# The edge stage of a graph layer in fp32: TensorE's products grouped by the shape that they take of the array, and vector messages that carry the zero score

## Chip, cores and metric

One core of one Trainium2 chip runs the whole program. The metric is the device time of one execution in microseconds (us), the median of several; lower is better. All tensors are fp32, and so are all TensorE products. Each of them leaves two records in the trace (a transpose leaves one), so 416 products of one kind stand there as x832.

## The reference, cut to what matters

A layer over a graph of 3125 nodes (256 features each) and 53125 edges that are sorted by their target node. It adds a message-passing block and a linear-attention block to `x`, and then a mixture of 8 experts. The change lies in the message-passing block alone. For each edge, after the linear maps are folded together:

```python
r  = edge_vector / |edge_vector|                     # 3 numbers for each edge
z  = [x0[src] , sum_m x1[src][:, m] * r[m]]          # 64 + 64 features of the source node
h  = z @ Wab                                         # 64 numbers, hidden scalars
sc = leaky_relu(h, 0.01) @ Wsc                       # 64 scores
act = softmax([sc, 0, 0, ... 0])                     # 256 wide: 192 scores are zero
msg[0:64]   = act[0:64] * (z @ Wo)[0:64]
msg[64:256] = act_zero  * ((z @ Wo)[64:128] (x) r + Q[src])   # one common zero score
agg[dst] += msg                                      # segment sum over the edges
```

The softmax has one common weight for its 192 zero scores. With `ex` the exponentials and `z` one over their sum, a scalar message has the factor `ex[u] * z`, and a vector message the factor `ex[U] * z`, where `ex[U]` is the exponential of the zero score (`U` is 64).

## The kernel before, in words

Three stages follow one another. Up to about 78 us the node table is written (`table`, 448 numbers a node: features and `Q`). From there to about 692 us runs the edge stage, `edges` (L762), which the change touches. The experts (`blocks`, L1253) follow to the end; their first block's products start as the edge stage ends.

The edge stage works on 104 groups of 4 x 128 edges. Group `s` goes through these functions, spread over four iterations of the loop at L947:

- `gather` (L786): four indirect DMAs issued by GpSimd (POOL) fetch the table rows of 512 source nodes into `xg`. Seven buffers; the gather runs three groups ahead.
- `features` (L810): three VectorE (DVE) operations build the second half of `z` in `xg`: `tmp<-xg`, `tmp<-tmp`, `xg<-tmp`.
- `places` (L794): `place`, a one-hot matrix of each edge's node in a window of 64 nodes.
- `turn` (L817): four TensorE transposes into `pz`, which ScalarE (ACT) copies to `zT`. These take all 128 rows and 128 columns of the array.
- `products` (L824): `ph` (the hidden scalars: 128 rows, 64 columns of the array, two products into the two halves of the partitions), from which ACT makes `little`, and `eo` (z @ Wo: four products of 128 x 128). `eo` has two PSUM buffers.
- `second_layer` (L840): `low` on DVE (the leaky relu), then four products `sc` (64 rows, 128 columns).
- `scores` (L853): `nm` on DVE, then four exponentials `ex` on ACT, with their sums in `z`.
- `messages` (L864): four small operations on `z`, then `zplace` on ACT (four operations, `place` times the zero weight) and `oplace` on DVE (`place` times `z`), then the messages `msg`, vectors (768 wide) and scalars (256 wide).
- `sums` (L894): products that add the messages into `ps`, 64 nodes x 256, for two halves of the partitions (128 rows, 64 columns). For each of two halves `b`: `msg`'s scalars with `oplace` (64 wide), `msg`'s vectors with `zplace` (192 wide), `Q` from `xg` with `zplace` (192 wide). In the first half of a window's first group all of `msg` goes with `oplace` in one product of 256 columns, because that product has to start the sum; for these tiles alone the vector messages are multiplied by `ex[U]` beforehand (`weight`, `re`).
- A window has three groups. At its end one product (`ps<-win,move`, L921) adds what the window before holds of this one, ACT copies the sum out (`win`, L929), and `second` (L934) does the same for the other half (64 rows, 64 columns). The `win` rows go to `agg` in HBM over SyncE's queue.

One iteration traces, in this order: `gather(s+3)`, `sums(s-3)`, a step of side work (attention, gate and planning of the experts: its products are named `gp`), `scores(s-2)`, `features(s)`, `places(s)`, `turn(s)`, `second_layer(s-1)`, `messages(s-2)`, `products(s)`, `second(s-3)`. The order on each engine is then set by a scheduler that takes what is ready first by its own estimates; `tc.issue_after(x)` binds it to put an instruction behind `x` on the same engine. It is an order of issue, not a wait. Before the change `ph(g)` is bound behind `sc(g-1)`, `sc(g)` behind the transposes of `g+1`, `low(g)` behind the features of `g+1`, and the `z` of `g` behind `low(g+1)`. The scheduler also splits the four transposes in two pairs in places.

Of the kernel before, what the change touches and what calls it, by code (L numbers as in the profile page):

```python
# [9 lines left out]
F32 = mybir.dt.float32  # L10
# [7 lines left out]
P = 128  # L18
# [8 lines left out]
def tile_gps_layer(  # L27
# [16 lines left out]
    nc = tc.nc  # L44
    N, D = x.shape
    NE = src.shape[0]
    U = 64
# [5 lines left out]
    G = 4  # L53
    JT = -(-NE // (P * G)) * G
    NG = JT // G
# [6 lines left out]
    TW = D + 3 * U  # L62
# [4 lines left out]
    W = 64  # L67
# [26 lines left out]
    ident = const.tile([P, P], F32, name="ident")  # L94
# [7 lines left out]
    wab = const.tile([P, U], F32, name="wab")  # L102
    wo = const.tile([P, 2 * U], F32, name="wo")
# [5 lines left out]
    r3 = const.tile([P, 3, JT], F32, name="r3")  # L109
# [40 lines left out]
    order = keep_.tile([P, EX], F32, name="order")  # L150
# [611 lines left out]
    def edges(gps):  # L762
        with tc.tile_pool(name="xgp", bufs=7) as xgp, tc.tile_pool(name="sp", bufs=5) as spool, \
# [5 lines left out]
                tc.tile_pool(name="sps", bufs=1, space=PSUM) as sps, \  # L769
                tc.tile_pool(name="gwork", bufs=1) as gw:  # L770
            XG, S, ZT, EO, MSG, WIN, SUM, MOVE = {}, {}, {}, {}, {}, {}, {}, {}
            READY_, HEAD, LOW, LSC, TURN, SC, M1 = {}, {}, {}, {}, {}, {}, {}
            ENDS = {}
            LAST = []
            both_sums = sps.tile([P, 2, D], F32, name="ps")
            WIN[-1] = spool.tile([P, D], F32, name="win", bufs=3)
            nc.gpsimd.memset(WIN[-1], 0.0)
            weight = spool.tile([P, G], F32, name="weight", bufs=1)
            nc.vector.memset(weight, 1.0)

            def pair(g):

                v = (g + 1) // 3
                return v, g - max(0, 3 * v - 1), 3 if v else 2
# [31 lines left out]

            def turn(g):  # L817
                pz = zps.tile([P, G, P], F32, name="pz")
                for i in range(G):
                    TURN[g] = nc.tensor.transpose(pz[:, i, :], XG[g][:, i, 0:P], ident)  # L820
                ZT[g] = ew.tile([P, G, P], F32, name="zT", bufs=3)
                nc.scalar.copy(ZT[g], pz)  # L822

            def products(g):  # L824

                zT = ZT.pop(g)
                ph = hps.tile([P, 2 * P], F32, name="ph")
                for h in range(2):
                    with tc.issue_after(LSC[g - 1].ins) if g and not h else nullcontext():
                        nc.tensor.matmul(ph[h * U:(h + 1) * U, :], lhsT=wab,  # L830
                                         rhs=zT[:, 2 * h:2 * h + 2, :].rearrange("p t e -> p (t e)"),
                                         start=True, stop=True)
                little = ew.tile([P, 2 * P], F32, name="little")
                nc.scalar.activation(little, ph, AF.Copy, scale=0.01)
                LOW[g] = ph, little
                EO[g] = eo = ops.tile([P, G, 2 * U], F32, name="eo")
                for t in range(G):
                    nc.tensor.matmul(eo[:, t, :], lhsT=zT[:, t, :], rhs=wo, start=True, stop=True)  # L838

            def second_layer(g):  # L840
                ph, little = LOW.pop(g)
                low = ew.tile([P, 2 * P], F32, name="low")
                with tc.issue_after(READY_[g + 1].ins) if g + 1 < NG else nullcontext():
                    LOW[g] = nc.vector.tensor_tensor(low, ph, little, OP.max)
                SC[g] = sc = cps.tile([P, G, 4 * U], F32, name="sc")
                with tc.issue_after(TURN[g + 1].ins) if g + 1 < NG else nullcontext():
                    for b in range(2):
                        for h in range(2):
                            hs = slice(h * U, (h + 1) * U)
                            LSC[g] = nc.tensor.matmul(sc[:, 2 * h + b, 0:U + 1], lhsT=low[hs, b * P:(b + 1) * P],  # L850
                                                      rhs=lsc[hs, :], start=True, stop=True)
# [9 lines left out]
                                         bias=nm[:, i:i + 1], accum_out=z[:, i:i + 1])  # L861
                HEAD[g] = ex, z

            def messages(g):  # L864
                eo, place = EO.pop(g), S.pop(g)
                ex, z = HEAD.pop(g)
                order = LOW[g + 1] if g + 1 < NG else None
                with tc.issue_after(order.ins) if order else nullcontext():
                    nc.vector.scalar_tensor_tensor(z, ex[:, :, U], float(3 * U - 1), z, op0=OP.mult, op1=OP.add)
                nc.vector.reciprocal(z, z)  # L870

                zero = ew.tile([P, G], F32, name="zero")
                nc.vector.tensor_mul(zero, z, ex[:, :, U])  # L873
                zero_place = spool.tile([P, G, W], F32, name="zplace", bufs=3)
                for i in range(G):
                    nc.scalar.activation(zero_place[:, i, :], place[:, i, :], AF.Copy, scale=zero[:, i:i + 1])  # L876
                one_place = spool.tile([P, G, W], F32, name="oplace", bufs=3)
                order = nc.vector.tensor_mul(one_place, place, z.unsqueeze(2).to_broadcast([P, G, W]))
                msg = ew.tile([P, G, D], F32, name="msg", bufs=3)
                rg = r3[:, :, g * G:(g + 1) * G].rearrange("p m g -> p g m")  # L880
                if pair(g)[1] == 0:

                    re = ew.tile([P, G, 3], F32, name="re")
                    nc.vector.tensor_copy(weight[:, 0:G:2], ex[:, 0:G:2, U])
                    nc.vector.tensor_mul(re, rg, weight.unsqueeze(2).to_broadcast([P, G, 3]))
                    rg = re
                with tc.issue_after(order.ins):
                    nc.vector.tensor_mul(msg[:, :, U:D].rearrange("p g (u m) -> p g u m", m=3),  # L888
                                         eo[:, :, U:2 * U].unsqueeze(3).to_broadcast([P, G, U, 3]),
                                         rg.unsqueeze(2).to_broadcast([P, G, U, 3]))  # L890
                nc.vector.tensor_mul(msg[:, :, 0:U], eo[:, :, 0:U], ex[:, :, 0:U])  # L891
                MSG[g] = msg, one_place, zero_place

            def sums(g):  # L894
                msg, one_place, zero_place = MSG.pop(g)
                v, q, n = pair(g)
                if q == 0:
                    SUM[v] = both_sums[:, v & 1, :]
                ps = SUM[v]
                xg = XG.pop(g)  # L900
                for b in range(2):

                    whole = q == b == 0
                    for what in range(3):
                        if whole and what == 1:
                            continue
                        for h in range(2):
                            i = 2 * h + b
                            hs = slice(h * W, (h + 1) * W)

                            with tc.issue_after(ENDS[v - 1].ins) if v and h and whole and not what else nullcontext():
                                if what == 0:
                                    c1 = D if whole else U
                                    nc.tensor.matmul(ps[hs, 0:c1], lhsT=one_place[:, i, :], rhs=msg[:, i, 0:c1],  # L914
                                                     start=whole, stop=False)
                                else:
                                    nc.tensor.matmul(ps[hs, U:D], lhsT=zero_place[:, i, :],  # L917
                                                     rhs=msg[:, i, U:D] if what == 1 else xg[:, i, D:TW],
                                                     start=False, stop=False)
                if q == n - 1:  # L920
                    nc.tensor.matmul(ps[0:W, :], lhsT=MOVE[v][:, 0, :], rhs=WIN.pop(v - 1),  # L921
                                     start=False, stop=True)
                    WIN[v] = spool.tile([P, D], F32, name="win", bufs=3)
                    close(v, 0)

# [8 lines left out]
            def second(g):  # L934
                v, q, n = pair(g)
                if q == n - 1:
                    ENDS[v] = nc.tensor.matmul(SUM[v][W:P, :], lhsT=MOVE.pop(v)[0:W, 1, :], rhs=WIN[v][0:W, :],  # L937
                                               start=False, stop=True)
                    close(v, 1)
                    del SUM[v]  # L940

# [5 lines left out]
            for s in range(NG + 3):  # L947
# [9 lines left out]
                    scores(s - 2)  # L957
                if s < NG:
                    features(s)
                    places(s)  # L960
                    turn(s)
                if 1 <= s < NG + 1:
                    second_layer(s - 1)
                if 2 <= s < NG + 2:
                    messages(s - 2)
                if s < NG:
                    products(s)
                if 3 <= s:
                    second(s - 3)

# [426 lines left out]
```

## Time and profile before

| | before |
|---|---|
| median of 3 runs | 1110.63 us (1109.84 to 1115.06) |
| profiled execution | 1108.81 us, span 1106.9 us, mean granted TensorE clock 0.964 |
| TensorE (PE) busy | 1018.8 us, 92% of the span |
| VectorE (DVE) busy | 698.7 us, 63% |
| ScalarE (ACT) busy | 500.6 us, 45% |
| GpSimd (POOL) busy | 630.3 us, 57% |
| first and last start of the transposes `pz` | 78.3 and 682.5 us |
| first and last start of the products `eo` | 81.2 and 685.7 us |

A row of the timeline names the start of a run of like instructions, the time from its start to its end, the engine, line and operation, the tiles and how many records the run has. Matmuls are pipelined, so the ends overlap with the next start: what a run costs TensorE is the difference between its start and the start of the run after it. That difference is called a stride here. DVE and ACT instructions overlap by some 0.08 us in the same way. An idle time is given in brackets with what ended it.

### The profile page before, as it was taken

How to read it: one execution, taken by the hardware profiler on the slowest of the kernel's cores; microseconds unless marked ns; L12 is line 12 of the kernel's file. 1: busy time of each engine (PE TensorE's matmuls, PEld its weight loads, DVE VectorE, ACT ScalarE, POOL GpSimd, SP SyncE). 2: the span in 40 equal slices, each digit the busy share in tenths (PEclk: the TensorE clock that was granted, in tenths of full speed). 3: DMA queues.
4: the chain of work that ended last, by engine and by line, in shares of the span. 5: the costliest groups of instructions: out<-in, count | busy, mean ns of one | idle time of the engine just before them, and what ended most of it. 6: DMA issues, size and time to landing. Idle time of an engine off the chain costs nothing.

```text
span 1106.9 us, 21729 instructions
## 1 busy us (share of the span) xinstructions
PE 1018.8 (92%) x7616; PEld 812.5 (73%) x7616; DVE 698.7 (63%) x2177; ACT 500.6 (45%) x1861; POOL 630.3 (57%) x623
## 2 busy tenths in 40 slices
PE   3848999999999999999999899899999999999996
PEld 3726776766667776776667676688888888888885
DVE  5987899988898989988888987322671111111110
ACT  3714556665576665765566545223211223222221
POOL 4447777777777776777766751432534434445322
PEclk9958999999999999999999899899999999999998
DMA  5945665667766686766766542765653667676651
GB/s 161 334 126 158 181 184 164 176 177 236 207 173 184 183 240 190 200 170 174 214 179 188 161 136 101 273 195 166 215 181 119 200 194 256 215 231 187 188 170 20
DMA packets 73882, 204.95 MB, mean 185 GB/s; under 512 B 13163, under 2 KB 48549, under 8 KB 70181
## 3 DMA queue, kind: packets, MB, share of 16 engines
q0 software_dynamic: 40736, 171.18, 52.9%
q1 hardware_dynamic: 31135, 30.40, 8.2%
q10 hardware_dynamic: 1894, 1.89, 0.5%
q8 instruction: 63, 1.03, 0.4%
q14 instruction: 54, 0.44, 0.1%
HBM read 176.00 MB, written 27.84 MB: 184 GB/s over the span
## 4 chain that ended last, share of the span: by engine, by line
PE 70%; DVE 12%; DMA 6%; issue 4%; POOL 3%; ACT 3%; SPq 0%; DVEq 0%; POOLq 0%; ACTq 0%
PE ps L1300 15%; PE ps L1318 15%; PE ps L917 8%; PE eo L838 7%; DMA xg<-table,srcT 4%; PE ph L830 4%; PE pz L820 3%; PE ps L914 3%; PE sc L850 3%; POOL xg L790 3%; PE gp L646 2%; PE gp L1095 2%; DVE tmp L813 2%; DVE msg L888 1%; PE ps L937 1%
## 5 line engine op out<-in xcount | busy, mean ns | idle before, releaser
L790 POOL DMA_INDIRECT xg<-table,srcT x416 | 441.1, 1060 | 163.5 <-issue 108.1
L876 ACT ACTIVATE zplace<-place,zero 128x64 f32<-128x64 f32 x416 | 115.3, 339 | 71.9 <-DVE zero L873 71.8
L838 PE MATMUL eo<-wo,zT 128*128 128x128 f32 x832 | 122.5, 292 | 25.3 <-DVE msg L891 24.9
L1305 ACT ACTIVATE hT<-ps,wt 128x256 f32<-128x256 f32 (+1 forms) x144 | 57.8, 453 | 194.3 <-issue 122.0
L838 PEld LDWEIGHTS eo<-wo,zT 128*128 128x128 f32 x832 | 105.4, 197 | 52.5 <-DVE msg L891 37.0
L860 ACT ACTIVATE ex<-sc,nm 128x65 f32<-128x65 f32 x416 | 125.5, 317 | 13.3 <-DVE nm L858 7.1
L1300 PE MATMUL ps<-xt,wt 128*128 128x256 f32 (+1 forms) x576 | 121.7, 368 | 4.4 <-DVE y L1321 4.4
L1318 PE MATMUL ps<-wt,hT 128*128 128x256 f32 x528 | 117.3, 379 | 0.0
L1300 PEld LDWEIGHTS ps<-xt,wt 128*128 128x128 f32 x576 | 103.4, 194 | 17.5 <-DVE y L1321 4.8
L813 DVE TENSOR_TENSOR tmp<-xg,r 128x768 f32<-128x768 f32 x104 | 98.7, 949 | 18.8 <-DMA xg<-table,srcT 15.4
L1318 PEld LDWEIGHTS ps<-wt,hT 128*128 128x128 f32 x528 | 98.8, 190 | 12.6
L917 PE MATMUL ps<-xg,zplace 128*64 128x192 f32 x832 | 107.5, 336 | 0.0
L1231 DVE COPY xt<-psx 128x512 f32<-128x512 f32 (+1 forms) x27 | 17.6, 651 | 140.1 <-PE psx L1230 133.2
L822 ACT COPY zT<-pz 128x512 f32<-128x512 f32 x104 | 60.7, 584 | 86.7 <-PE pz L820 85.1
L1323 POOL DMA_INDIRECT out_dram<-y,ridx_late x32 | 51.0, 1594 | 76.8 <-DVE y L1321 48.8
L917 PE MATMUL ps<-msg,zplace 128*64 128x192 f32 x692 | 91.4, 342 | 0.0
L860 ACT ACTIVATION_READ_ACCUMULATOR ex<-sc,nm 128x1 f32 x416 | 86.3, 208 | 0.0
L1323 POOL DMA_INDIRECT out_dram<-y,ridx_early x20 | 32.3, 1614 | 87.9 <-DVE y L1321 33.6
L820 PE MATMUL pz<-ident,xg 128*128 128x128 f32 x416 | 69.6, 288 | 10.4 <-DVE xg L815 8.1
L914 PE MATMUL ps<-msg,oplace 128*64 128x64 f32 (+1 forms) x832 | 78.4, 268 | 0.6 <-DVE msg L891 0.6
L820 PEld LDWEIGHTS pz<-ident,xg 128*128 128x128 f32 x416 | 45.3, 143 | 41.3 <-issue 32.9
L830 PE MATMUL ph<-zT,wab 128*64 128x256 f32 x416 | 69.0, 409 | 6.0 <-ACT zT L822 3.0
(383 smaller groups left out, 1898.3 us busy)
## 6 DMA issues: line engine op xcount, KB each, us to landing
xg<-table,srcT POOLq DMA_INDIRECT x416, 3.7
table<-xt SPq DMA_DIRECT2D x4, 1120.0 KB
agg<-win SPq DMA_DIRECT2D x70, 64.0 KB
agg<-zero SPq DMA_DIRECT2D x1, 3200.0 KB
x<-in_x_dram SPq DMA_DIRECT2D x2, 768.0 KB
at<-agg SPq DMA_DIRECT2D x2, 768.0 KB
out_dram<-x SPq DMA_DIRECT2D x2, 768.0 KB
rows<-at SPq DMA_DIRECT2D x2, 768.0 KB
```

What stands on the lines that cost most here:

```text
L790: nc.gpsimd.indirect_dma_start(out=XG[g][:, i, :], out_offset=None, in_=table[:, :], in_offset=bass.IndirectOffsetOnAxis(ap=srcT[:, j:j + ...
L813: nc.vector.tensor_mul(tmp, xg[:, :, U:D].rearrange("p g (m u) -> p g m u", m=3), rbc(g))
L820: TURN[g] = nc.tensor.transpose(pz[:, i, :], XG[g][:, i, 0:P], ident)
L830: nc.tensor.matmul(ph[h * U:(h + 1) * U, :], lhsT=wab, rhs=zT[:, 2 * h:2 * h + 2, :].rearrange("p t e -> p (t e)"), start=True, stop=True)
L838: nc.tensor.matmul(eo[:, t, :], lhsT=zT[:, t, :], rhs=wo, start=True, stop=True)
L860: nc.scalar.activation(ex[:, i, :], sc[:, i, 0:U + 1], AF.Exp, scale=-1.0, bias=nm[:, i:i + 1], accum_out=z[:, i:i + 1])
L876: nc.scalar.activation(zero_place[:, i, :], place[:, i, :], AF.Copy, scale=zero[:, i:i + 1])
L914: nc.tensor.matmul(ps[hs, 0:c1], lhsT=one_place[:, i, :], rhs=msg[:, i, 0:c1], start=whole, stop=False)
L917: nc.tensor.matmul(ps[hs, U:D], lhsT=zero_place[:, i, :], rhs=msg[:, i, U:D] if what == 1 else xg[:, i, D:TW], start=False, stop=False)
L1300: nc.tensor.matmul(ps[:, h, 0:W_], lhsT=w[:, k * HID + cc * P:k * HID + (cc + 1) * P], rhs=xT[:, k, 0:W_], start=(k == 0), stop=(k == 1))
L1318: nc.tensor.matmul(ps, lhsT=hT[:, cc, s * P:(s + 1) * P], rhs=w[:, o:o + D], start=(cc == 0), stop=(cc == NC - 1))
L1323: nc.gpsimd.indirect_dma_start(out=out[:, :], out_offset=bass.IndirectOffsetOnAxis(ap=ridx[q][:, at_], axis=0), in_=y[:, s, :], in_offset= ...
```

## The change

- `products(g)` moves one iteration later, behind `sums` and ahead of `turn`. The new bonds make TensorE's order in an iteration: `sums(s-3)` (all with 64 columns of the array), `ph(s-1)` (64 columns too), `eo(s-1)`, transposes of `s` (both 128 x 128), `sc(s-1)`, and at a window's end `second(s-3)` behind `sc`.
- `messages` is cut in two. `weights(g)` makes `z`, `zplace` and `oplace`; `messages(g)` makes `msg`. The `z` of `g` is bound behind the features of `g+2` (before: behind `low(g+1)`), and `low(g)` behind `oplace` of `g-1` (before: behind the features of `g+1`). So on DVE `oplace` of a group now stands ahead of the next group's `low`.
- All vector messages are multiplied by `ex[U]` beforehand: `re` is made for every tile of every group (one operation of 12 columns, 104 times; before 35 times, with a copy into `weight`).
- `sums` then has one product of 256 columns for each tile (`oplace` with all of `msg`) and one of 192 (`zplace` with `Q`), in place of 64, 192 and 192. `zplace` is still made, for `Q`.
- `places` moves to the end of the iteration.

```diff
             def turn(g):
                 pz = zps.tile([P, G, P], F32, name="pz")
-                for i in range(G):
-                    TURN[g] = nc.tensor.transpose(pz[:, i, :], XG[g][:, i, 0:P], ident)
+                with tc.issue_after(WO[g - 1].ins) if g else nullcontext():
+                    for i in range(G):
+                        TURN[g] = nc.tensor.transpose(pz[:, i, :], XG[g][:, i, 0:P], ident)
...
             def products(g):
...
-                    with tc.issue_after(LSC[g - 1].ins) if g and not h else nullcontext():
-                        nc.tensor.matmul(ph[h * U:(h + 1) * U, :], lhsT=wab,
...
+                    with tc.issue_after(SUMS[g - 2].ins) if g >= 2 and not h else nullcontext():
+                        first = nc.tensor.matmul(ph[h * U:(h + 1) * U, :], lhsT=wab,
...
                 for t in range(G):
-                    nc.tensor.matmul(eo[:, t, :], lhsT=zT[:, t, :], rhs=wo, start=True, stop=True)
+                    with tc.issue_after(first.ins) if not t else nullcontext():
+                        WO[g] = nc.tensor.matmul(eo[:, t, :], lhsT=zT[:, t, :], rhs=wo, start=True, stop=True)
 
             def second_layer(g):
...
-                with tc.issue_after(READY_[g + 1].ins) if g + 1 < NG else nullcontext():
+                with tc.issue_after(PLACED[g - 1].ins) if g else nullcontext():
                     LOW[g] = nc.vector.tensor_tensor(low, ph, little, OP.max)
...
-            def messages(g):
-                eo, place = EO.pop(g), S.pop(g)
-                ex, z = HEAD.pop(g)
-                order = LOW[g + 1] if g + 1 < NG else None
-                with tc.issue_after(order.ins) if order else nullcontext():
+            def weights(g):
+                place = S.pop(g)
+                ex, z = HEAD[g]
+                with tc.issue_after(READY_[g + 2].ins) if g + 2 < NG else nullcontext():
                     nc.vector.scalar_tensor_tensor(z, ex[:, :, U], float(3 * U - 1), z, op0=OP.mult, op1=OP.add)
...
-                order = nc.vector.tensor_mul(one_place, place, z.unsqueeze(2).to_broadcast([P, G, W]))
+                PLACED[g] = nc.vector.tensor_mul(one_place, place, z.unsqueeze(2).to_broadcast([P, G, W]))
+                MSG[g] = one_place, zero_place
+
+            def messages(g):
+                eo = EO.pop(g)
+                ex, z = HEAD.pop(g)
+                one_place, zero_place = MSG.pop(g)
+                order = LOW[g + 1] if g + 1 < NG else PLACED[g]
                 msg = ew.tile([P, G, D], F32, name="msg", bufs=3)
-                rg = r3[:, :, g * G:(g + 1) * G].rearrange("p m g -> p g m")
-                if pair(g)[1] == 0:
-
-                    re = ew.tile([P, G, 3], F32, name="re")
-                    nc.vector.tensor_copy(weight[:, 0:G:2], ex[:, 0:G:2, U])
-                    nc.vector.tensor_mul(re, rg, weight.unsqueeze(2).to_broadcast([P, G, 3]))
-                    rg = re
+                re = ew.tile([P, G, 3], F32, name="re")
+                nc.vector.tensor_mul(re, r3[:, :, g * G:(g + 1) * G].rearrange("p m g -> p g m"),
+                                     ex[:, :, U:U + 1].to_broadcast([P, G, 3]))
...
             def sums(g):
...
-                    whole = q == b == 0
-                    for what in range(3):
...
+                    for h in range(2):
+                        i, hs = 2 * h + b, slice(h * W, (h + 1) * W)
+
+                        with tc.issue_after(ENDS[v - 1].ins) if v and h and q == b == 0 else nullcontext():
+                            nc.tensor.matmul(ps[hs, :], lhsT=one_place[:, i, :], rhs=msg[:, i, :],
+                                             start=(q == b == 0), stop=False)
+                    for h in range(2):
+                        i, hs = 2 * h + b, slice(h * W, (h + 1) * W)
+                        SUMS[g] = nc.tensor.matmul(ps[hs, U:D], lhsT=zero_place[:, i, :], rhs=xg[:, i, D:TW],
+                                                   start=False, stop=False)
...
             def second(g):
...
+                    with tc.issue_after(LSC[g + 2].ins) if g + 2 < NG else nullcontext():
+                        ENDS[v] = nc.tensor.matmul(SUM[v][W:P, :], lhsT=MOVE.pop(v)[0:W, 1, :],
+                                                   rhs=WIN[v][0:W, :], start=False, stop=True)
...
                 if s < NG:
                     features(s)
-                    places(s)
+                if 2 <= s < NG + 2:
+                    weights(s - 2)
+                if 1 <= s < NG + 1:
+                    products(s - 1)
+                if s < NG:
                     turn(s)
                 if 1 <= s < NG + 1:
                     second_layer(s - 1)
                 if 2 <= s < NG + 2:
                     messages(s - 2)
                 if s < NG:
-                    products(s)
+                    places(s)
                 if 3 <= s:
                     second(s - 3)
```

More of the change, by code (lines that the diff above doesn't have):

```diff
@@ L771, in edges @@
             XG, S, ZT, EO, MSG, WIN, SUM, MOVE = {}, {}, {}, {}, {}, {}, {}, {}
-            READY_, HEAD, LOW, LSC, TURN, SC, M1 = {}, {}, {}, {}, {}, {}, {}
+            READY_, HEAD, LOW, LSC, TURN, SC, WO, PLACED, SUMS = {}, {}, {}, {}, {}, {}, {}, {}, {}
             ENDS = {}
@@ L777, in edges @@
             nc.gpsimd.memset(WIN[-1], 0.0)
-            weight = spool.tile([P, G], F32, name="weight", bufs=1)
-            nc.vector.memset(weight, 1.0)
             def pair(g):
@@ L828, in products @@
                 for h in range(2):
-                    with tc.issue_after(LSC[g - 1].ins) if g and not h else nullcontext():
-                        nc.tensor.matmul(ph[h * U:(h + 1) * U, :], lhsT=wab,
-                                         rhs=zT[:, 2 * h:2 * h + 2, :].rearrange("p t e -> p (t e)"),
-                                         start=True, stop=True)
+                    with tc.issue_after(SUMS[g - 2].ins) if g >= 2 and not h else nullcontext():
+                        first = nc.tensor.matmul(ph[h * U:(h + 1) * U, :], lhsT=wab,
+                                                 rhs=zT[:, 2 * h:2 * h + 2, :].rearrange("p t e -> p (t e)"),
+                                                 start=True, stop=True)
                 little = ew.tile([P, 2 * P], F32, name="little")
@@ L889, in messages @@
                                          eo[:, :, U:2 * U].unsqueeze(3).to_broadcast([P, G, U, 3]),
-                                         rg.unsqueeze(2).to_broadcast([P, G, U, 3]))
+                                         re.unsqueeze(2).to_broadcast([P, G, U, 3]))
                 nc.vector.tensor_mul(msg[:, :, 0:U], eo[:, :, 0:U], ex[:, :, 0:U])
@@ L901, in sums @@
                 for b in range(2):
-                    whole = q == b == 0
-                    for what in range(3):
[L905 to L919, printed above, removed]
+                    for h in range(2):
[7 more added lines that the diff above has]
+                                                   start=False, stop=False)
                 if q == n - 1:
-                    nc.tensor.matmul(ps[0:W, :], lhsT=MOVE[v][:, 0, :], rhs=WIN.pop(v - 1),
-                                     start=False, stop=True)
+                    SUMS[g] = nc.tensor.matmul(ps[0:W, :], lhsT=MOVE[v][:, 0, :], rhs=WIN.pop(v - 1),
+                                               start=False, stop=True)
                     WIN[v] = spool.tile([P, D], F32, name="win", bufs=3)
@@ L936, in second @@
                 if q == n - 1:
-                    ENDS[v] = nc.tensor.matmul(SUM[v][W:P, :], lhsT=MOVE.pop(v)[0:W, 1, :], rhs=WIN[v][0:W, :],
-                                               start=False, stop=True)
+                    with tc.issue_after(LSC[g + 2].ins) if g + 2 < NG else nullcontext():
+                        ENDS[v] = nc.tensor.matmul(SUM[v][W:P, :], lhsT=MOVE.pop(v)[0:W, 1, :],
+                                                   rhs=WIN[v][0:W, :], start=False, stop=True)
                     close(v, 1)
```

## Prediction

> **What bounds the kernel now.** I read the windows first (which engine is full in the edge stage), then TensorE's timeline (what one group costs there), then the chain of waits, the gathers' own view, and the waits.
>
> ```profile
> 78.00:200.00 122.00, 114.28 (x1004) 85.43 (x1004) 105.71 (x306) 66.96 (x279) 94.70 (x89) 0.96 0.63 173
> 200.00:264.00 64.00, 62.61 (x614) 44.31 (x612) 57.90 (x167) 42.64 (x181) 48.49 (x47) 1.00 0.64 175
> 264.00:505.00 241.00, 227.75 (x2139) 166.66 (x2140) 211.50 (x674) 151.32 (x638) 182.45 (x173) 0.98 0.69 199
> 505.00:692.00 187.00, 173.81 (x1587) 127.91 (x1587) 159.36 (x548) 106.27 (x457) 109.45 (x106) 0.95 0.57 163
> ```
>
> Behind the length stand PE, PEld, DVE, ACT and POOL busy, then the granted clock. TensorE is busy 93 to 98% of every part and DVE 85 to 90%; DVE's durations overlap by 0.08 us, so it has more room than that. TensorE is the first bound. Its timeline, between 214 and 222 us, where no side work runs:
>
> ```profile
> 214.16 1.06 PE L838 MATMUL eo<-wo,zT 128*128 128x128 f32 x8
> 215.15 0.65 PE L914 MATMUL ps<-msg,oplace 128*64 128x256 f32 x4
> 215.63 0.50 PE L917 MATMUL ps<-xg,zplace 128*64 128x192 f32 x4
> 215.96 0.28 PE L914 MATMUL ps<-msg,oplace 128*64 128x64 f32 x4
> 216.07 0.50 PE L917 MATMUL ps<-msg,zplace 128*64 128x192 f32 x4
> 216.40 0.50 PE L917 MATMUL ps<-xg,zplace 128*64 128x192 f32 x4
> 216.82 0.44 PE L820 MATMUL pz<-ident,xg 128*128 128x128 f32 x2
> ...
> 218.75 1.16 PE L838 MATMUL eo<-wo,zT 128*128 128x128 f32 x8
> 219.84 0.34 PE L914 MATMUL ps<-msg,oplace 128*64 128x64 f32 x4
> ```
>
> Strides: the same 192-column run with `xg` takes 0.325 us where a run of the same shape follows (215.63 to 215.96) and 0.42 where the transposes follow (216.40 to 216.82). `eo` takes 0.99 behind the transposes (214.16 to 215.15) and 1.09 behind `ph` (218.75 to 219.84). Leaving a shape of the array costs 0.10, entering one 0.05 (a 64-column run takes 0.165 behind `eo` and 0.114 behind its like; 0.10 for `eo`). That is what the change is after.
>
> But TensorE is not the bound everywhere. In the chain of waits between 440 and 480 us the gathers stand on the path:
>
> ```profile
> 463.27 5.12 DMA xg<-table,srcT
> 468.43 3.45 DMA xg<-table,srcT
> 474.14 3.23 DMA xg<-table,srcT
> ```
>
> ```profile
> L790 POOL DMA_INDIRECT xg<-table,srcT x416: 941/949/2322, 66.9 to 657.7; - x139
>   issue: 108.1, 313
>   PE pz L820: 17.0, 24
> ```
>
> A gather's instruction lasts 0.95 us at best, 1.06 on average, with 0.305 us of idle ahead of every one: 1.365 us, 5.46 for a group, 568 us for all 104. Idle beyond those 0.305 (waits for a free `xg` buffer) comes to only 24.2 us, added up along POOL's timeline, 8.3 of it before group 71. At groups 71, 73 and 75 (472, 483 and 494 us) DVE's first operation starts the moment the gather lands: there the stage is as late as POOL makes it.
>
> ```profile
> PE eo L838 <- DVE msg L891: 24.9, 21, 3.8
> DVE z L869 <- ACT ex L860: 18.3, 31, 1.7
> ```
>
> These waits, TensorE for the messages and DVE for the exponentials, are the ones that the new order moves.
>
> **The change, part by part.**
>
> Fewer shapes. In the order in which the builds issue, TensorE changes the shape 555 times in the edge stage before and 392 times after. At 0.10 + 0.05 us the 163 that go are worth 24.5 us. [...]
>
> Wider product. 64 and then 192 columns (0.114 + 0.328) become 256: 0.482 behind `eo` (215.15 to 215.63), so 0.432 behind its like. That saves 0.010 for each of 173 half groups (208 less the 35 that have it already): 1.7 us. [...] I take 1.7.
>
> So TensorE's own work falls by 26 us, 0.25 for a group. Summed along its timeline from 86 to 690 us (603.6 us) it has some 549 us of strides without a wait and 54 of waits and of half-speed clock behind them; 549 becomes 523.
>
> DVE: `re` for 69 more groups at 0.057 us is +3.9, 35 copies less at 0.07 is -2.5. 1.4 us at most lands on the path; TensorE covers it wherever DVE idles. `zplace` stays, ACT's work and the number of DMAs stay; POOL's queue and SyncE's keep their order. The `win` copy of `second` now stands behind `sc`.
>
> The new loop. `low(s)` is now behind `oplace(s-1)`, which needs the exponentials of `s-1`, which need `sc(s-1)`. From `nm`: it ends after 0.43, ACT starts 0.09 later, four exponentials 1.29, 0.04 to DVE, then `z`, `re`, one step of the features, reciprocal, another step, `zero`, `oplace` 1.27 (strides), `low` 0.33, the messages 1.20, and the next `nm`: 4.65 us. In the shadow of the exponentials DVE has `place` and `tmp`, 1.18 us, so it idles 0.34 (side work or `move` fill that). TensorE needs 1.56 (`sums`) + 0.53 + 0.99 + 0.53 + 0.59 = 4.21, at a window's end 1.0 more, so 4.55 on average and 5.04 with the side work (523 / 104). Side work adds 0.47 to DVE's loop: its strides in the stage come to 502 us where none waits, 104 x 4.36 = 453 of them for the edges, and 49 / 104 = 0.47. That makes 5.1. The two are level. Queued behind a late `z` are `low` and `msg`; TensorE waits for `low` at `sc` and, some 0.6 us, for `msg` at the next `sums`, in place of the present wait of `eo` for `msg`. No trace shows this loop at work. From both sides: nothing, as side work and the gathers fill the same time, or 0.3 us for a group, 31 us, if the smaller of both ends adds up. The nearest row is the present wait of `eo` (24.9), which goes; I set what comes against what goes, and the net at 1.
>
> The gathers. `sums(s-3)`, which frees a buffer, keeps its place in the iteration. Up to group 75 TensorE's 75 x 0.25 = 19 us cannot come out: POOL can be earlier there only by the 8.3 us that it waited for buffers. I take 8.3. After group 75 the gathers lead by 3.4 to 17.7 us, and 28 x 0.25 = 7 come out.
>
> Clock. Half-speed stretches of 3.4 us (1.7 lost each) follow idle times of 1.2 to 2.9 us of TensorE in this trace, though 5 others of 1.1 to 1.6 had none; seven lie in the stage after 250 us. [...] I count no change, and 1.7 us for each one more or less.
>
> Sum: -8.3 - 7.0 + 1 + about 0.5 for `re` = -14 against the profiled execution's 1108.8: 1094.8. The median of the runs lies 1.8 above it: 1096.6, said as 1096.5.
>
> **The rivals.**
>
> *The loop sets the pace.* Slower. Side work on TensorE and on DVE hangs together (a `gp` product waits for DVE and DVE for it), so in a serial loop both add: 4.65 + 0.47 + 0.60 (TensorE's side work, 63 us / 104) + 0.19 (`second`, 0.57 every third group, now between `sc` and `sums`) = 5.91 for a group, against 5.80 measured (603.6 / 104): 104 x 0.11 = +11 us, 1121.6. It decides where more than 1.15 us comes on top of 4.65. For it: DVE waits for `ex` 31 times already. Against: in the attention stretch side work comes in stride with 0.65 us of DVE, and there TensorE still has the longer sum.
>
> *The gathers do not hold it.* If POOL's instructions are as short as their best where DVE is idle more, or the lead at group 75 can shrink, all 26 us come out: 1084.6; with a few of the 54 us of waits 1079. For it: the transposes stand 7 us and more behind the first DVE operation at groups 71 to 75, so there is lead to use. Against: DVE works in order, and `tmp` of two groups ahead stands in front of `z`, so a late gather stops all of it.
>
> *Nothing comes out.* The waits for buffers stay (TensorE frees them at the same pace), the gates wait for rows of `agg` as now (the chain shows 4.4 us for such a load at 533 us), and new waits eat the rest: 1105 to 1114.
>
> **How the numbers follow.** A difference of 0.5%, 5.5 us, is about what the runs can tell from none. First case 0.50 (1088 to 1103), no hold by the gathers 0.20, nothing 0.15, loop 0.15. Faster by over 0.5%: 0.50 + 0.20 + 0.01 = 0.71; within: 0.14; slower: 0.15. The range from 1079 to 1114 leaves out the loop's case and a little below.
>
> **What would show it.** Right: runs of the 192-column `xg` product at 0.325 ahead of `ph`; `eo` at 0.99; `sc` followed by `sums` or by the second `win` product; `ps<-msg,oplace` 256 wide with 208 runs; no idle time of `eo` for `msg`, some of `sums` for it; POOL's extra idle below 24 us; more starts of `tmp` at the very landing. The loop: idle time of `sc` for `low` or of DVE for `ex` of over 60 us, groups without side work at 4.7 or more with POOL waiting for buffers. Wrong from the start, if strides between the same shapes differ from 0.325, or if the first `eo` to the last takes as long as now (604 us).

## Result, and the profile after

The change makes the kernel slower: 1200.0 us against 1112.0 us, ratio 1.080 with a 95% interval of 1.076 to 1.085. The prediction said 1096.5 us, in a range of 1079 to 1114. The profiled execution has a span of 1197.9 us and a mean granted clock of 0.93 (0.96 before). All of the loss lies in the edge stage: the last product of its last window ends at 788.7 us in place of 697.1, and what follows takes 409.2 us in place of 409.8.

The windows of the stage come first, with PE, PEld, DVE, ACT and POOL busy, then the clock, the DMA share and GB/s.

```profile
130.00:200.00 70.00, 64.63 (x544) 47.69 (x542) 63.54 (x195) 41.41 (x174) 55.07 (x50) 0.98 0.62 169
200.00:264.00 64.00, 46.96 (x364) 32.78 (x362) 43.57 (x125) 29.61 (x127) 42.66 (x41) 0.89 0.56 152
264.00:505.00 241.00, 197.71 (x1554) 142.29 (x1556) 182.23 (x582) 128.32 (x537) 144.59 (x142) 0.90 0.58 165
505.00:780.00 275.00, 230.94 (x1816) 168.16 (x1814) 204.68 (x696) 144.85 (x598) 148.60 (x144) 0.89 0.52 147
```

Up to 200 us little is wrong (in the same 70 us TensorE was busy 67.1 us before). From there every engine falls together: TensorE from 92% to 73%, DVE from 91% to 68%, POOL from 79% to 67%, and the clock with them. When no engine is full, several of them may be waiting in a ring. The waits between 100 and 700 us name its members (us in total, times, longest):

```profile
DVE tmp L811 <- DMA xg<-table,srcT: 105.8, 53, 6.2
...
PE sc L850 <- DVE low L844: 82.9, 33, 6.1
...
POOL xg L788 <- PE ps L912: 76.4, 29, 8.0
```

DVE waits for gathered rows, TensorE for DVE's `low`, and POOL for the sums on TensorE to release a buffer, so that it can gather. The same three before:

```profile
DVE tmp L813 <- DMA xg<-table,srcT: 10.4, 9, 2.1
...
POOL xg L790 <- PE ps L917: 9.2, 9, 2.3
...
PE sc L850 <- DVE low L844: 0.3, 1, 0.3
```

The timeline (start, duration, engine, line; in brackets the idle time before and what ended it) shows one turn, with ACT, the weight loads and the other steps left out:

```profile
247.29 0.96 DVE L811 TENSOR_TENSOR tmp<-xg,r 128x768 f32<-128x768 f32 x1 [3.01 <-DMA xg<-table,srcT]
...
249.52 0.41 DVE L844 TENSOR_TENSOR low<-ph,little 128x256 f32<-128x256 f32 x1
...
249.99 0.66 PE L850 MATMUL sc<-lsc,low 64*128 64x65 f32 x8 [3.50 <-DVE low L844]
...
251.19 1.12 PE L908 MATMUL ps<-msg,oplace 128*64 128x256 f32 x4 [0.53 <-DVE msg L893]
...
254.75 1.03 POOL L788 DMA_INDIRECT xg<-table,srcT  x1 [4.33 <-PE ps L912]
...
262.28 0.96 DVE L811 TENSOR_TENSOR tmp<-xg,r 128x768 f32<-128x768 f32 x1 [3.57 <-DMA xg<-table,srcT]
```

By counting the groups from the first, these are `tmp` of group 30, `low` and `sc` of group 26, the sums of group 25, the gather of group 32 into the buffer that group 25 releases, and `tmp` of group 32. From the first line to the last the stage moves on by two groups and takes 15.0 us, 7.5 us a group, where the kernel before needs 5.8. What matters here is which group's `low` stands behind which group's `tmp`.

I call that the lead: by how many groups `tmp` (a group's first operation, the one that waits for its gather) stands ahead of `low` in DVE's order of issue. Of the 104 groups:

| kernel | lead 0 | 1 | 2 | 3 | 4 |
|---|---|---|---|---|---|
| before | 1 | 78 | 25 | - | - |
| after | 1 | 4 | 26 | 28 | 45 |

The change binds `z(g)` behind `READY[g+2]` and `low(g+1)` behind `oplace(g)`. That sets a least lead and no greatest one. The scheduler then puts `tmp` three groups ahead from group 24 on (211 us) and four from group 28 on (232 us), in the stretch where the windows turn bad.

With B buffers and a lead of L, `tmp(k)` stands ahead of `low(k-L)`. Behind that `low` come `sc(k-L)` and the sums of group k-L-1. They release the buffer that the gather of group k-L-1+B takes, and its `tmp` begins the next turn. So a turn moves on by B-L-1 groups: 7-4-1 = 2 here, and 4 or 5 before. I call this theory A. The rival, theory B, is the one of the prediction: the serial loop through `nm`, `ex`, `z`, `oplace`, `low`, `sc` is the new bound, and the gathers are late only because TensorE is.

### The profile page after: what moved, and what is told of

It is laid out like the page before. It is cut to its first block, busy times and chain, and to the rows that moved or that the text cites. A ratio compares the mean times of both kernels' runs of the same rounds, so it can differ in the third digit from the quotient of the medians.

```text
span 1197.9 us, 20360 instructions
## 1 busy us (share of the span) xinstructions
PE 1032.5 (86%) x6924; PEld 819.3 (68%) x6924; DVE 704.5 (59%) x2210; ACT 507.5 (42%) x1861; POOL 626.6 (52%) x623
## 5 line engine op out<-in xcount | busy, mean ns | idle before, releaser
L788 POOL DMA_INDIRECT xg<-table,srcT x416 | 437.2, 1051 | 255.0 <-issue 105.0
L908 PE MATMUL ps<-msg,oplace 128*64 128x256 f32 x832 | 152.4, 449 | 25.6 <-DVE msg L893 15.2
L811 DVE TENSOR_TENSOR tmp<-xg,r 128x768 f32<-128x768 f32 x104 | 99.2, 954 | 112.7 <-DMA xg<-table,srcT 111.2
L875 ACT ACTIVATE zplace<-place,zero 128x64 f32<-128x64 f32 x416 | 110.2, 337 | 103.8 <-DVE zero L872 103.4
L850 PE MATMUL sc<-lsc,low 64*128 64x65 f32 x832 | 74.5, 301 | 83.4 <-DVE low L844 82.9
L850 PEld LDWEIGHTS sc<-lsc,low 64*128 64x128 f32 x832 | 59.4, 202 | 104.3 <-DVE low L844 94.6
L912 PE MATMUL ps<-xg,zplace 128*64 128x192 f32 x832 | 119.0, 369 | 0.0
L890 DVE TENSOR_TENSOR msg<-eo,re 128x768 f32<-128x768 f32 x104 | 98.3, 945 | 0.0
L912 PEld LDWEIGHTS ps<-xg,zplace 128*64 128x64 f32 x832 | 68.6, 158 | 41.1 <-issue 17.8
L908 PEld LDWEIGHTS ps<-msg,oplace 128*64 128x64 f32 x832 | 57.1, 154 | 56.9 <-DVE msg L893 22.9
L829 PE MATMUL ph<-zT,wab 128*64 128x256 f32 x416 | 82.0, 415 | 0.8 <-issue 0.8
```

The costliest lines, as they stand in the source:

```text
L788: nc.gpsimd.indirect_dma_start(out=XG[g][:, i, :], out_offset=None, in_=table[:, :], in_offset=bass.IndirectOffsetOnAxis(ap=srcT[:, j:j + ...
L811: nc.vector.tensor_mul(tmp, xg[:, :, U:D].rearrange("p g (m u) -> p g m u", m=3), rbc(g))
L829: first = nc.tensor.matmul(ph[h * U:(h + 1) * U, :], lhsT=wab, rhs=zT[:, 2 * h:2 * h + 2, :].rearrange("p t e -> p (t e)"), start=True, st ...
L908: nc.tensor.matmul(ps[hs, :], lhsT=one_place[:, i, :], rhs=msg[:, i, :], start=(q == b == 0), stop=False)
L912: SUMS[g] = nc.tensor.matmul(ps[hs, U:D], lhsT=zero_place[:, i, :], rhs=xg[:, i, D:TW], start=False, stop=False)
```

## Experiments

The kernels of each set ran on one chip, the kernel before among them. e5 to e8 and e13 to e16 stood on chips where the kernel before takes 1110.0 and 1111.4 us, e1 to e4 and e9 to e12 on others where it takes 1180.7 and 1192.6. So ratios to the kernel before on the same chip are compared, and the first two groups are told first, since they decide.

### The changed kernel, with an eighth buffer, with a bounded lead

```diff
 # e5: the changed kernel
 # e6: one more buffer (place: 3 buffers, zT: 2, to make room)
-tc.tile_pool(name="xgp", bufs=7)
+tc.tile_pool(name="xgp", bufs=8)
 # e7: as e6, and in features(g)
+with tc.issue_after(LOW[g - 5].ins) if g >= 5 else nullcontext():
     nc.vector.tensor_mul(tmp, ...)
 # e8: seven buffers, and in features(g)
+with tc.issue_after(LOW[g - 3].ins) if g >= 3 else nullcontext():
     nc.vector.tensor_mul(tmp, ...)
```

Expected of e5: 

> The changed kernel once more, unaltered, so that it stands on one chip beside its variants. Theory A (a ring of gathers: tmp of a group leads low by up to four groups in VectorE's order, so that a gather's buffer comes free too late): 1.07 to 1.09 of the kernel before, VectorE's tmp idle for gathers 100 us or more. Theory B (the loop nm, ex, z, oplace, low, sc sets the pace, and the gathers are only late because TensorE is): the same ratio.

Expected of e6: 

> Eight buffers for gathered rows in place of seven (two small pools one buffer smaller to make room). The emitted order then lets tmp lead low by up to five groups. Theory A: a turn of the ring advances by buffers less lead less one, 8-5-1 = 2 groups as in the changed kernel with 7-4-1 = 2, so little comes of it: 0.97 to 1.01 of the changed kernel, tmp still idle for gathers over 70 us. A rival (too few buffers): the extra buffer takes half of the loss away, ratio to the kernel before below 1.05. Theory B: no change.

Expected of e7: 

> Eight buffers as in the run beside it, and tmp of a group bound behind low of five groups before, so that it leads by four at most. Theory A: a turn advances by 8-4-1 = 3 groups in place of 2, some 15 us for 3 groups = 5 us a group, below what the other work takes: tmp's idle time for gathers falls below 40 us, and the time to 0.94 to 0.97 of the run with eight buffers alone. Theory B and the rival of too few buffers: within 1% of the run with eight buffers alone.

Expected of e8: 

> The changed kernel with tmp bound to lead low by two groups at most (as in an earlier run), now beside the changed kernel on one chip. Theory A: 0.93 to 0.97 of the changed kernel, tmp idle for gathers under 10 us. Theory B: within 1% of the changed kernel, and TensorE's sc idle for low as long as before.

| kernel | buffers, largest lead | groups a turn | us | ratio to before (95%) |
|---|---|---|---|---|
| e5 | 7, 4 | 2 | 1203.3 | 1.085 (1.080 to 1.090) |
| e6 | 8, 5 | 2 | 1200.7 | 1.081 (1.075 to 1.087) |
| e7 | 8, 4 | 3 | 1119.1 | 1.008 (1.004 to 1.012) |
| e8 | 7, 2 | 4 | 1104.1 | 0.995 (0.993 to 0.998) |

The group of `tmp` on the pages of e6, e7 and e8 in this order (busy and mean ns, then the idle time before it and what ended most of it; the added line moves L811 to L812, and for e8 the operation's own view is shown):

```profile
L811 DVE TENSOR_TENSOR tmp<-xg,r 128x768 f32<-128x768 f32 x104 | 99.1, 955 | 106.2 <-DMA xg<-table,srcT 106.2
```

```profile
L812 DVE TENSOR_TENSOR tmp<-xg,r 128x768 f32<-128x768 f32 x104 | 98.8, 951 | 36.3 <-DMA xg<-table,srcT 35.5
```

```profile
L812 DVE TENSOR_TENSOR tmp<-xg,r x104: 926/953/1007, 76.4 to 670.4; 128x768 f32<-128x768 f32 x104
its engine sat idle before it (us, times) until:
  DMA xg<-table,srcT: 19.6, 13
```

An eighth buffer brings nothing, since the scheduler spends it on a fifth group of lead (42 of the 104 groups): 8-5-1 is 2 again. The same eight buffers with one bond more take 82 us less. And with seven buffers and a lead of two all of the loss goes, while the loop of theory B stays whole. Theory A holds, B falls, and so does "too few buffers". The gain was larger than I expected: e8 takes 0.917 of e5's time (0.93 to 0.97 expected) and e7 0.932 of e6's (0.94 to 0.97). And `tmp` still waits 19.6 us for gathers in e8, where I expected under 10.

### A lead of three, the old order of low, half of the gathers

e14 is e8 again; e15 has `LOW[g - 4]` in its place. In e13 the lead is two and the old bonds of `low` and `z` are back:

```diff
 # e13, against e8
-with tc.issue_after(PLACED[g - 1].ins) if g else nullcontext():
+with tc.issue_after(READY_[g + 1].ins) if g + 1 < NG else nullcontext():
     LOW[g] = nc.vector.tensor_tensor(low, ph, little, OP.max)
...
-with tc.issue_after(READY_[g + 2].ins) if g + 2 < NG else nullcontext():
+with tc.issue_after(LOW[g + 1].ins) if g + 1 < NG else nullcontext():
     nc.vector.scalar_tensor_tensor(z, ...)
 # the loop calls weights(s - 2) just ahead of messages(s - 2) again
 # e16, against e8: bufs=4, and three constant tiles for the odd groups
 def gather(g):
+    if g % 2:
+        XG[g] = STILL[g // 2 % 3]
+        return
```

Expected of e13: 

> Lead of two with the old order of low and z, beside the lead of two alone. If the loop through low, z and oplace costs what the prediction charged (1 us net): within 0.5% of the lead of two alone. If that loop is the bound once the gathers are not: 1.5% or more faster than it. If the old order was better for another reason (low no longer late): TensorE's wait of sc for low gone, 0.5 to 1.5% faster.

Expected of e14: 

> The lead of two alone, as the run that the others of this call are held against: 0.995 of the kernel before where nothing else disturbs the engines (1.027 where, as on the chip of the first runs, the kernel before itself takes 1180 us).

Expected of e15: 

> Lead of three at most with seven buffers: 7-3-1 = 3 groups to a turn of some 15 us, 5 us a group, below the 5.9 us that a group takes in the kernel before: theory A gives 1.000 to 1.015 of the kernel before (the lead of four with eight buffers, also 3 groups a turn, gave 1.008). A loss that grows evenly with the lead would give 1.03 to 1.05.

Expected of e16: 

> Lead of two with only every second group's rows gathered (the odd groups work on three constant tiles, so this part of the computation is left out, the routing behind it differs, and only the edge stage is compared). If the pace of the gathers (5.5 us a group) holds the lead of two at a stage of 617 us, the stage falls to 570 to 600 us. If it stays at 610 to 625 us, TensorE and VectorE with the side work hold it.

| kernel | us | ratio to before (95%) |
|---|---|---|
| e14, lead 2 | 1104.1 | 0.994 (0.992 to 0.996) |
| e15, lead 3 | 1117.5 | 1.006 (1.004 to 1.008) |
| e13, lead 2, old order of `low` | 1127.2 | 1.014 (1.012 to 1.016) |

A lead of three with seven buffers (7-3-1 = 3 groups a turn) stands where a lead of four with eight stood (8-4-1 = 3): 1.006 and 1.008. Evenly with the lead it would have been near 1.04. So the loss is a threshold: three groups in 15 us, 5.0 a group, is below what a group takes anyway (5.9); two groups in 15 us is not. The 15 us are those of the one turn shown above.

e13 is 2% slower than e14, which none of its three cases had. So nothing here shows the loop to be the bound with a lead of two. But e13 does not price the loop either, because the old order brings a wait of its own: TensorE waits for `oplace` at the sums (between 100 and 700 us), and `sc` still waits 11.5 us for `low`:

```profile
PE ps L909 <- DVE oplace L878: 25.8, 41, 1.5
```

In e14 there is no such wait, so the change's place for `oplace`, ahead of `low`, is worth having.

e16 bears on why a lead of two gains 0.6% and not more. It leaves out the gathers of the odd groups, and ran once. Its routing differs behind the stage, so I compare the end of the stage alone, by the last `ps<-win` product (last start, 64 columns). e14 first, then e16:

```profile
L933 PE MATMUL ps<-win,move x70: 376/402/428, 105.5 to 696.4; 64*64 64x256 f32 x70
```

```profile
L940 PE MATMUL ps<-win,move x70: 376/402/427, 104.5 to 677.7; 64*64 64x256 f32 x70
```

With half of the gathers the stage takes 595.4 us in place of 619.1 (it begins 5 us later, as the tiles are filled first). So the gathers hold the kernel with a lead of two, as they were said to hold the changed kernel. Whether they do so by POOL's pace or by their traffic is not separated: in the stage the DMA moves 106 GB/s in e16 and 179 in e14. A single gather is hardly shorter where DVE idles more: DVE is busy for 87% of the stage before and 76% after the change, and a gather lasts 1060 and 1051 ns on average.

TensorE over the stage, from the first transposes to the end of the last window, before, after, in e14 and in e16 (length, then PE, PEld, DVE, ACT and POOL busy, the clock, the DMA share and GB/s):

```profile
78.30:697.10 618.80, 582.94 (x5375) 427.04 (x5375) 537.41 (x1698) 368.31 (x1557) 436.59 (x414) 0.97 0.63 179
77.60:788.70 711.10, 596.61 (x4683) 433.19 (x4683) 543.08 (x1732) 374.44 (x1557) 433.93 (x413) 0.90 0.55 156
77.70:696.80 619.10, 565.63 (x4683) 415.64 (x4683) 540.68 (x1732) 375.05 (x1557) 441.17 (x414) 0.96 0.63 179
82.70:678.00 595.30, 553.02 (x4682) 408.17 (x4681) 537.64 (x1725) 373.65 (x1557) 219.43 (x207) 0.98 0.37 106
```

The table splits the stage into three: what the half-speed clock costs (an estimate: half of TensorE's busy time in the stretches that were granted half of the clock), the rest of its busy time, and its idle time.

| kernel | stage | busy at full clock | clock | idle |
|---|---|---|---|---|
| before | 618.8 | 564.7 | 18.2 | 35.8 |
| after | 711.1 | 536.7 | 59.9 | 114.5 |
| e14, lead 2 | 619.1 | 541.7 | 23.9 | 53.5 |
| e16, half of the gathers | 595.4 | 541.4 | 11.7 | 42.3 |

### The same tests earlier, on the other chips

e1 is e8's kernel, e2 has `LOW[g - 2]` (lead 1). e3 is the kernel before with a lead of four, e4 the kernel before with only the wide product and `re` for all groups:

```diff
 # e3, against before
-with tc.issue_after(READY_[g + 1].ins) if g + 1 < NG else nullcontext():
+with tc.issue_after(READY_[min(g + 4, NG - 1)].ins):
     LOW[g] = nc.vector.tensor_tensor(low, ph, little, OP.max)
 # and features is called three groups earlier in the loop
```

Expected of e1: 

> The changed kernel with one bond more: the first features operation of group g is bound behind low(g-3), so tmp runs at most 2 groups ahead of low (in the changed kernel 2 to 4). Theory A (ring of gathers: tmp(g+4) stands ahead of low(g) on DVE, low gates sc and with it sums, sums frees the buffer for a gather, so 7 buffers advance only 6 less lead = 2 groups for each turn of some 14.7 us): the loss goes, tmp's idle time for the gathers falls from 111 us below 30, time 1085 to 1110. Rival B (the serial loop nm, ex, z, oplace, low, sc is the pace): no change, 1180 to 1205, idle time of sc for low stays near 170 us. Rival C (half-speed clock from TensorE's gaps, whatever makes them): 1150 to 1180.

Expected of e2: 

> The same with the bond behind low(g-2): tmp at most 1 group ahead of low. Theory A: as with a lead of 2 or up to 10 us slower (features then stand on the way to the next low), 1085 to 1120. Rival B: 1180 to 1205. Rival C: 1150 to 1180.

Expected of e3: 

> The kernel before with nothing of the change, but features traced three groups earlier and low(g) bound behind the features of g+4: tmp runs 4 groups ahead of low (before: 1 or 2). Theory A: slow like the changed kernel, 1170 to 1230, tmp idle for gathers 80 us and more. Rivals B and C: nothing of the new loop is in it, so 1105 to 1120.

Expected of e4: 

> The kernel before with the wide product alone (re for all groups, oplace with all of msg in 256 columns, no product of msg with zplace), its order bonds kept. All theories: the merge is worth little, -1.7 us on TensorE and up to +1.4 on DVE, 1106 to 1114.

| kernel | us (before: 1180.7) | ratio to before (95%) |
|---|---|---|
| e1, lead 2 | 1209.5 | 1.027 (1.018 to 1.036) |
| e2, lead 1 | 1211.5 | 1.024 (1.016 to 1.033) |
| e3, before with lead 4 | 1413.7 | 1.198 (1.189 to 1.207) |
| e4, before with the merge | 1189.9 | 1.007 (1.002 to 1.011) |

All four lie outside the times I expected, which were thought for a chip where the kernel before takes 1110 us. As ratios, too, e1 and e2 are slower than theory A allows (1.00 and 1.01 at most) and e3 far slower than its 1.05 to 1.11. With the lead at two or one DVE's `tmp` waits for gathers no longer (2.5 and 2.7 us in all, 111 in the changed kernel), but 2.4 to 2.7% stay here, and by their times alone e1 and e2 come nearest to theory B. Its other sign is missing: `sc` waits for `low` for 50 us in e1, counting the weight loads, where B had near 170 (177.5 in the changed kernel). The changed kernel itself was not run on this chip, so what the bound lead gives back here is not known. e3 needs no part of the change to lose more than the change did. Its page:

```profile
L790 POOL DMA_INDIRECT xg<-table,srcT x416 | 421.5, 1013 | 491.2 <-PE ps L917 233.4
L813 DVE TENSOR_TENSOR tmp<-xg,r 128x768 f32<-128x768 f32 x104 | 99.6, 958 | 261.8 <-DMA xg<-table,srcT 261.1
```

Here the lead is four in 100 groups, not in 45, and the same two waits are more than doubled (80.8 and 111.2 us in the changed kernel). So the ring arises with the old shapes and the old order of TensorE too. How much of the 20% it makes is open: 134 us of TensorE's idle time there (between 70 and 800 us) stand before the transposes, and the profile names nothing that they wait for.

Four more ran on a chip of the same kind (before: 1192.6): e9 is e13's kernel, e10 is e16's, e12 is e15's. e11 is a lead of two with the wide product split again:

```diff
 # e11, against e8, except in a window's first tiles
-nc.tensor.matmul(ps[hs, :], lhsT=one_place[:, i, :], rhs=msg[:, i, :], ...)
+nc.tensor.matmul(ps[hs, 0:U], lhsT=one_place[:, i, :], rhs=msg[:, i, 0:U], ...)
+nc.tensor.matmul(ps[hs, U:D], lhsT=one_place[:, i, :], rhs=msg[:, i, U:D], ...)
```

Expected of e9: 

> tmp leading low by two groups, and the new order of VectorE's work undone: low is bound behind READY of the next group and z behind low of the next, as in the kernel before, so that low no longer waits for oplace. If the loop nm, ex, z, oplace, low, sc costs what the prediction charged (1 us net, bounds 0 to 31), 0.985 to 1.003 of the kernel before, like the run with the lead alone (0.995). If the loop is the new bound once the gathers are not, 0.965 to 0.98.

Expected of e10: 

> tmp leading low by two groups, and only every second group's rows gathered: the odd groups work on three tiles filled once with 0.5 (this part of the computation is left out), the even ones have four buffers. If the pace of the gathers' descriptors on GpSimd (104 groups of 4 at 5.5 us a group) holds the run with the lead alone at 0.995, then 0.95 to 0.98 of the kernel before, the stage near 104 x 5.1 + side work; if TensorE or VectorE holds it, 0.99 to 1.0.

Expected of e11: 

> tmp leading low by two groups, and the wide 256-column product split again into 64 and 192 columns for all tiles but a window's first, in the same order, so only the merging is undone. By the prediction's 1.7 us on TensorE: 0.995 to 0.999 of the kernel before. If the extra pass costs as much as the per-row price of a half group seems (0.43 against 0.13 + 0.33 us), nothing beyond 0.5%; over 1.005 would mean that the merging was worth more than counted.

Expected of e12: 

> The changed kernel with tmp bound to lead low by three groups at most. Theory A: a turn of the ring advances by 7-3-1 = 3 groups, as with eight buffers and a lead of four (1.008): 1.000 to 1.015 of the kernel before, between the lead of two (0.995) and that of four (1.085), and far nearer to the lead of two. If the loss grew evenly with the lead: 1.03 to 1.05.

They missed their forecasts too: 1.024 (e9), 1.026 (e11) and 1.026 (e12), each with an interval of about 0.005 to either side, and 1.010 for e10, which takes some 80 us longer behind the stage, its routing being another. Together with e1 and e2, all variants of the changed kernel with a lead of three or less and all gathers lie at 1.024 to 1.027 there, whatever else they do. Something other than the ring holds them, and so e9, e11 and e12 tell nothing of what they were made for. The traces show a part of it: in e1, e2, e4, e9, e11 and e12 TensorE idles 23 to 41 us between 100 and 680 us with no wait that the profile names, and DVE 24 to 32 us for signals that come from no instruction shown. On the other chips the first is 4 us at most and the second does not occur. The largest such waits of TensorE in e4, which has nothing of the new order, and in e12:

```profile
PE ph L828 <- issue: 17.1, 17, 1.6
```

```profile
PE ps L909 <- issue: 23.9, 24, 2.6
```

"Issue" stands for no wait that shows. What the wide product alone is worth stays open: e4's 0.7% loss stands on such a chip, and e11's comparison with it.

## Why the prediction was wrong, step by step

**The step that failed** is "The gathers. `sums(s-3)`, which frees a buffer, keeps its place in the iteration." The sums did keep their place. The change moved the other end, DVE's `tmp`, against `low`, and I did not count it. The step needed one more number, the lead in DVE's order, and it was there to be counted before any run: 1 or 2 before, up to 4 after. With seven buffers that is two groups a turn. Its own rule named the mechanism ("DVE works in order, and `tmp` of two groups ahead stands in front of `z`, so a late gather stops all of it"), but used it only against a rival. The trace of after shows it: `little` of group 26 is ready at 245.45 us, and DVE, idle for 3.01 us, starts `low` of that group only at 249.52, behind `tmp` of group 30, whose gather lands at 247.29. The forecast that POOL's idle time beyond 0.305 us a gather stays below 24 us came out at 117.6. In place of 14 us less, the ring of late gathers made the kernel 88 us slower (1112.0 to 1200.0).

**TensorE's shapes: right.** The timeline of after, with the strides read from start to start:

```profile
258.49 0.65 PE L908 MATMUL ps<-msg,oplace 128*64 128x256 f32 x4 [0.46 <-ACT win L923]
...
258.97 0.49 PE L912 MATMUL ps<-xg,zplace 128*64 128x192 f32 x4
...
259.29 0.60 PE L908 MATMUL ps<-msg,oplace 128*64 128x256 f32 x4
...
259.72 0.49 PE L912 MATMUL ps<-xg,zplace 128*64 128x192 f32 x4
...
260.05 0.60 PE L829 MATMUL ph<-zT,wab 128*64 128x256 f32 x4
...
260.58 1.16 PE L838 MATMUL eo<-wo,zT 128*128 128x128 f32 x8
...
261.58 0.60 PE L819 MATMUL pz<-ident,xg 128*128 128x128 f32 x4
```

The wide product takes 0.48 after another shape and 0.43 after its like, the 192-column run 0.32 and 0.33 ahead of `ph`, `ph` 0.53, `eo` 1.00. Each was forecast within 0.01. The sum was 26 us less of TensorE's own work; the table above has 564.7 - 541.7 = 23.0 in e14, and 28.0 in the changed kernel.

**The hold by the gathers: right in kind.** With the lead taken back, 7 us came out (1111.4 to 1104.1) where the sum had 14. The rival in which the gathers do not hold it gave 26 less; e16, with half of them, has a stage 23 us shorter than before. In e14's profiled execution (1108.3 us, where the median of its runs is 1104.1) neither the 8.3 us up to group 75 nor the 7 behind it show: the gather of group 75 starts at 489.0 us (486.7 before) and the last `eo` at 685.9 (685.7). The shapes save 23.0 us there, and 17.7 us more of idle time and 5.7 of clock eat them. TensorE's waits name most of that idle time (e14, between 100 and 700 us):

```profile
PE sc L851 <- DVE low L845: 21.0, 16, 6.4
PE ps L909 <- DVE msg L894: 11.2, 23, 2.1
PE ps L909 <- ACT win L924: 9.5, 20, 0.9
```

Before, in the same stretch, these three were 0.3, 0.6 and 0.4 us, and `eo` waited 21.2 us for `msg`, which it does no longer.

**The clock: wrong by 42 us.** "I count no change" was an estimate that no run shows. In the trace of before, eight idle times of TensorE of 0.41 to 0.62 us (between 100 and 697 us) have no half-speed stretch behind them. But in the changed kernel `sc` alone waits for `low` 2.5 us on average (82.9 us in 33 waits), and TensorE's clock is at half speed for 139 us of the stage (38 before), worth 59.9 us in place of 18.2. It went back with the ring: with the lead at two the half-speed time is 49 us in e8 and 54 in e14. So the 92 us of loss are 79 of idle time and 42 of clock, less 28 of work saved (rounded).

**The loop: not the cause of the loss, its price open.** The prediction set what comes against what goes "and the net at 1". By e14's waits above, 32.2 - 0.9 = 31.3 us came and 21.2 went, some 10 us net. The late gathers have a share in it (with half of them, in e16, `sc` waits 12.4 us for `low`), so what the loop alone costs is not shown. The wait of the sums for the `win` copy, 9 us more, was put at nothing. The loop's sign, TensorE's `sc` idle for `low` over 60 us, did appear in the changed kernel (82.9), but it had another cause: `low` was late as DVE stood at `tmp`, and with the lead at two 62 us of it are gone with the loop unchanged. A forecast's sign must be one that only its own mechanism gives.

**The rival on the slower side** was 1121.6; the outcome, 78 us above that, was in none of the cases.

## What to carry to other kernels

When an order of work changes, count on each engine that keeps its order, as DVE did here, how far the operation that waits for a transfer stands ahead of the one that lets a buffer go, and compare that with the number of buffers: a turn moved on by buffers less lead less one here. Bound the lead from above where bonds bound it only from below; one such line gave back 99 us here (e5 to e8), and more buffers without it gave nothing. Engines that all fall together from one point on are a hint of such a ring, not a proof: e1's TensorE idles 114.8 us in the stage, as much as in the changed kernel (114.5), while DVE's `tmp` waits 2.5 us for gathers in all. The sign is the pair of waits, the first operation for its gather and the gather for its buffer.

## What the runs showed of the hardware that I had not expected

- The kernel before differs by 6 to 7% from chip to chip (each chip was used once, so the chip and the hour are not told apart): 1110 to 1112 us in the first comparison and on the chips of e5 to e8 and e13 to e16, 1181 and 1193 on the other two. On the latter the stage alone is longer, and e10, with half of the gathers, keeps a stage of 625.6 us there, where e12, with all of them, has 737.2; on a chip of the other kind the same two kernels have 595.4 and 620.2 (e16, e15). Outside the stage the profiled span of e12 has 487.7 us and that of e15 486.8. The waits that the profile does not name shrink with the gathers there too (TensorE 38 us in e12, 8 in e10); what makes them stays open.
- More stalls came with less clock: in the changed kernel TensorE idles 114.5 us in the stage, in place of 35.8, and its clock is at half speed for 139 us, in place of 38, which is worth some 42 us more (an estimate: 59.9 less 18.2).
